# Exchanging score groups and moving a token norm in the written-out order of an attention kernel

## The chip, the cores and the metric

The kernel runs on one core of one Trainium2 chip. The metric is the device time of one execution in microseconds (us); lower is better. Before the change the median of three runs is 799.85 us (798.22 to 801.39).

## What is computed

The input `x` is 4 batches of 2048 tokens with 256 channels, in float32. Two sandwiches are applied, one after the other:

```python
x = x + layernorm(attention(layernorm(x)))
x = x + layernorm(ffn(layernorm(x)))
```

Attention has one head of width 256: `q, k, v = split(x @ weight_qkv)`, scores `q k^T / 16`, a softmax over the 2048 keys, the product with `v`, an output projection and a bias. The second part mixes each token with its predecessor, takes `r = sigmoid(xr W_r)` and `k = relu(xk W_k)^2`, and returns `r * (k W_v)`.

## The kernel before

**Tiling.** The 8192 tokens are cut into 32 blocks of 256 tokens, numbered g, eight to a batch. A block is two tiles of 128 tokens; in most names `j` or `i` is the tile (0 or 1). The keys of a batch are 2048, and scores are made for 128 queries by 1024 keys at a time, so that a block has four score groups: tile `i`, half `h` of the keys. Half 0 comes from the first two chunks of 512 tokens of the batch, half 1 from the other two.

**Precision.** Float32 operands are split into two float16 parts, high and low (`...H` and `...L`), and a product is the sum of three matmuls, or two where one operand has no low part. The weights of q and k are multiplied together ahead of time (`GH`, `GL`), and the first thing made for a block is therefore `t`, the normed tokens times that product.

**Operations.** Each short word in the strings `HEAD`, `LOOP` and `TAIL` calls one small function with a block number. `sM@0/1/0` is `sM` for the current block with tile 1 and half 0; `pj@-2` is `pj` for the block two before. `run` (L914) calls them in the order of the words, and under `manual_schedule` (L922) each engine gets its own instructions in that order. So the string is the order of work of every engine, and of the DMA queue of SP. A word that is written later than another holds up only words on its own engine, and those that wait for its data or its buffer. `HEAD` fills the pipeline, `LOOP` is called for blocks 3 to 26, and `TAIL` empties it.

In one turn of `LOOP` for block g the words that matter here are these.

- Next block's `t`: `tM@1` (TensorE, L350, 10 matmuls into the tile `tps`), `tH@1` (ScalarE, L362, high part), `tL@1` (VectorE, L368, low part `tps - tH`).
- Scores of block g: `sM` (TensorE, L377, 10 matmuls per group, with `tH` and `tL` of the block as the weights that are loaded), `sX` (VectorE, L394, maximum of a group), `sB` (VectorE, L399, the bias of the exponential from the maxima of both halves, so it needs both groups of a tile), `sE` (ScalarE, L406, the exponential and its sum), `sH` (ScalarE, L413), `sL` (VectorE, L419), `sT` (DMA transpose from SP, L425, which writes a quarter of `PT`).
- Product with the values of the block before: `pv@-1/0/8` and `pv@-1/8/16` (TensorE, L432, 40 matmuls each). The first reads the half 0 quarters of `PT`, the second the half 1 quarters. Then `zH` (ScalarE), `zL` (VectorE, L465), which feed `pj` (TensorE, L471), `y` (VectorE, L483), and the statistics `bS` (VectorE), `bP` (GpSimd), the norm `bN` (ScalarE) and `bA` (GpSimd, L526).
- Second part for blocks two to five before: `hF`, `hN`, `hX`, `hT`, `hO`, `hD`, `mk`, `mr`, `kM`, `kR`, `kA`, `uH`, `uL`, `rM`, `rT`, `oM`, `yy`, `dS`, `dP`, `dN`, `dA`, `st`.
- Tokens of blocks ahead: `aS@9` (VectorE, statistics), `aP@9` (GpSimd), `aN@9` (L314, the normed tokens as float16, two instructions of 128x256), `aM@9` and `aD@9` (GpSimd, the low part), `aT@8` (DMA transpose from SP, one turn later).

**Buffers.** Scores lie in two PSUM buffers (`ps_s`), so a group waits until the exponential has read the group that had the buffer before. `tps`, `op`, `k`, `r` and `o` share two more (`ps_m`).

Of the kernel before, what the change touches and what calls it, by code (L numbers as in the profile page):

```python
# [51 lines left out]
sT@2/1/1 pv@1/8/16  # L52
"""
LOOP = """
sM@0/0/0 yy@-5 sM@0/0/1 aS@9 zH@-2 dS@-5 hF@-3/act/act zL@-2 dP@-5 sX@0/0/1 kM@-4 pj@-2 dn@-2
pv@-1/0/8 sX@0/0/0 sB@0/0 hN@-3/act/act y@-2 tM@1 aP@9 sM@0/1/0 dN@-5/act/act sM@0/1/1 aN@9/pool
hX@-3/pool kR@-4 dA@-5/pool aT@8 bS@-2 hC@-3 kA@-4 sE@0/0/0 sE@0/0/1 bP@-2 sH@0/0/0 sH@0/0/1 hT@-3
sL@0/0/0 bN@-2/act/act rM@-4 hO@-3/dve sL@0/0/1 tH@1 aL@11 pv@-1/8/16 hD@-3/pool ld@0 sT@0/0/1
aM@9/pool uH@-4 sX@0/1/0 sX@0/1/1 rT@-4 bA@-2/pool sB@0/1 sE@0/1/0 mk@-3 kH@-3 sH@0/1/0 cS@-2
uL@-4/pool sE@0/1/1 oM@-4 sH@0/1/1 tL@1 sL@0/1/0 sT@0/0/0 mr@-3 sL@0/1/1 st@-5 kL@-3/pool sT@0/1/0  # L60
rH@-3 rL@-3/pool sT@0/1/1 aD@9/pool cP@-2
"""
TAIL_BLOCKS = 5
TAIL = """
# [907 lines left out]
```

## Time and profile before

| | |
|---|---|
| median of three runs | 799.85 us |
| the profiled execution | 798.83 us, of which the profile's span is 797.0 us |
| TensorE (PE) busy | 781.7 us, 98% |
| VectorE (DVE) busy | 696.9 us, 87% |
| ScalarE (ACT) busy | 536.3 us, 67% |
| GpSimd (POOL) busy | 464.6 us, 58% |
| granted TensorE clock, mean | 0.997 |

Times in the profile are counted from the start of the span. A turn of `LOOP` in the middle of the kernel is one period of 23.70 us on every engine; the one from 401.72 to 425.42 us is used as the sample. The first turn (block 3) has its first score matmul near 73 us and the second turn near 93 us; the last turn ends at 638.86 us. In lists of instructions the columns are the start, the length, the engine, the line of the kernel, the operation, output and inputs, shapes and how many were merged; in brackets stands how long the engine sat idle before, and what ended that.

### The profile page before, as it was taken

What the parts mean: (1) busy time and instruction counts of PE and PEld (TensorE: products, weight loads), DVE (VectorE), ACT (ScalarE), POOL (GpSimd) and SP (SyncE); (2) the same over time, 40 slices, a digit from 0 to 9 for tenths busy, and PEclk for the clock granted to TensorE, in tenths of its full rate; (3) what the DMA queues carried; (4) which work ended last, traced back from release to release, by engine and by line L of the source; (5) the groups of instructions that cost most, each with busy time, mean ns of one, the idle gap of its engine ahead of it and who ended that gap; (6) DMA issues with size and microseconds to landing.
All of it is one profiled execution on the core that took longest, in us unless ns stands there. A gap on an engine that the chain in (4) does not pass through costs nothing.

```text
span 797.0 us, 15916 instructions
## 1 busy us (share of the span) xinstructions
PE 781.7 (98%) x5803; PEld 574.3 (72%) x5803; DVE 696.9 (87%) x1606; ACT 536.3 (67%) x889; POOL 464.6 (58%) x632
## 2 busy tenths in 40 slices
PE   8999999999999999999999999999999999999995
PEld 6467677777777777777777777777777767777784
DVE  7998888898888888888888988888898989999977
ACT  6666676686667677667677667668576756575754
POOL 4034457757666766666766766775545534445696
PEclk9999999999999999999999999999999999999998
DMA  8778866556755647664758775656655553655521
GB/s 238 178 146 172 148 153 145 139 133 143 155 141 134 154 119 143 155 157 119 168 117 140 145 169 124 139 118 128 143 123 120 119 119 61 139 122 130 144 71 66
DMA packets 351199, 109.18 MB, mean 137 GB/s; under 512 B 324624, under 2 KB 351120, under 8 KB 351120
## 3 DMA queue, kind: packets, MB, share of 16 engines
q1 hardware_dynamic: 350848, 107.91, 61.1%
q8 instruction: 45, 0.74, 0.4%
q14 instruction: 34, 0.28, 0.1%
q10 hardware_dynamic: 272, 0.26, 0.1%
HBM read 18.75 MB, written 8.39 MB: 34 GB/s over the span
## 4 chain that ended last, share of the span: by engine, by line
PE 90%; DVE 5%; DMA 1%; ACT 1%; issue 1%; POOL 0%; POOLq 0%; SPq 0%; ACTq 0%; DVEq 0%
PE z L442 33%; PE s L173 33%; DMA PT__995<-hl__1240 1%; DMA xa__110<-in_x_dram 1%; PE warm__211 L806 0%; PE op__11019 L173 0%; PE warm__520 L806 0%; PE k__11262 L173 0%; DVE x__10522 L247 0%; DVE sm L818 0%; PE o__11191 L173 0%; PE op__10541 L173 0%; DVE mxmx__10570 L396 0%; DVE pstsA__150 L254 0%; PE r__10479 L173 0%
## 5 line engine op out<-in xcount | busy, mean ns | idle before, releaser
L173 PEld LDWEIGHTS <-w_kH 128*128 128x128 f16 x248 | 24.3, 98 | 8.2 <-issue 0.5
L173 PEld LDWEIGHTS <-GH 128*128 128x128 f16 x192 | 18.8, 98 | 3.7 <-DVE tL__334 L372 0.7
L442 PEld LDWEIGHTS <-X__271 128*128 128x128 f16 x160 | 15.7, 98 | 2.2
L442 PEld LDWEIGHTS <-X__6669 128*128 128x128 f16 x160 | 15.7, 98 | 2.2
L442 PEld LDWEIGHTS <-X__5273 128*128 128x128 f16 x160 | 15.6, 98 | 2.2
L442 PEld LDWEIGHTS <-X__189 128*128 128x128 f16 x160 | 15.5, 98 | 2.3 <-issue 0.5
L442 PEld LDWEIGHTS <-X__233 128*128 128x128 f16 x160 | 15.7, 98 | 1.8
L442 PEld LDWEIGHTS <-X__718 128*128 128x128 f16 x160 | 15.7, 98 | 1.8
L442 PEld LDWEIGHTS <-X__324 128*128 128x128 f16 x160 | 15.7, 98 | 1.8
L442 PEld LDWEIGHTS <-X__4575 128*128 128x128 f16 x160 | 15.7, 98 | 1.8
L442 PEld LDWEIGHTS <-X__571 128*128 128x128 f16 x160 | 15.7, 98 | 1.8
L442 PEld LDWEIGHTS <-X__1783 128*128 128x128 f16 x160 | 15.7, 98 | 1.8
L442 PEld LDWEIGHTS <-X__3179 128*128 128x128 f16 x160 | 15.7, 98 | 1.8
L442 PEld LDWEIGHTS <-X__7367 128*128 128x128 f16 x160 | 15.7, 98 | 1.8
L442 PEld LDWEIGHTS <-X__3877 128*128 128x128 f16 x160 | 15.7, 98 | 1.8
L442 PEld LDWEIGHTS <-X__1141 128*128 128x128 f16 x160 | 15.7, 98 | 1.8
L442 PEld LDWEIGHTS <-X__2481 128*128 128x128 f16 x160 | 15.7, 98 | 1.8
L442 PEld LDWEIGHTS <-X__5971 128*128 128x128 f16 x160 | 15.6, 98 | 1.8
L173 PEld LDWEIGHTS <-GL 128*128 128x128 f16 x128 | 12.5, 98 | 3.4 <-issue 0.9
L173 PEld LDWEIGHTS <-w_kL 128*128 128x128 f16 x124 | 12.1, 98 | 1.4
L329 POOL TENSOR_TENSOR X__718<-xa__485,X__718 128x256 f16<-128x256 f32 x1 | 1.7, 1657 | 16.4 <-ACT xa__485 L271 16.4
L273 POOL TENSOR_SCALAR xa__344<-xa__344,rsrna__455,nmrna__456 128x128 f32<-128x128 f32 x2 | 0.9, 449 | 17.2 <-ACT X__571 L271 17.2
(3619 smaller groups left out, 3383.6 us busy)
## 6 DMA issues: line engine op xcount, KB each, us to landing
xa__103<-in_x_dram SPq DMA_DIRECT2D x1, 256.0 KB, 3.3
scr_wk__101<-in_wkT_dram ACTq DMA_DIRECT2D x1, 256.0 KB, 3.8
xa__110<-in_x_dram SPq DMA_DIRECT2D x1, 256.0 KB, 4.2
xa__112<-in_x_dram SPq DMA_DIRECT2D x1, 256.0 KB, 4.5
scr_wq__114<-in_wqT_dram SPq DMA_DIRECT2D x1, 256.0 KB, 4.7
scr_wv__130<-in_wvT_dram SPq DMA_DIRECT2D x1, 256.0 KB, 4.9
xa__163<-in_x_dram SPq DMA_DIRECT2D x1, 256.0 KB, 5.2
xa__175<-in_x_dram SPq DMA_DIRECT2D x1, 256.0 KB, 5.4
```

The lines of the kernel that those rows point to most:

```text
L173: nc.tensor.matmul(out_ap, l, r, start=(i == 0), stop=(i == len(pairs) - 1))
L273: eng(e).tensor_scalar(dst, src, rs[:, j:j + 1], nm[:, j:j + 1], ALU.mult, ALU.add)
L329: eng(e).tensor_tensor(Xh[:, :, 2, :], T["xa", g][:, :, P:D], Xh[:, :, 1, :], ALU.subtract)
L442: nc.tensor.matmul(z[:, int(c), 0:QB], a, p, start=(kt == 0 and n == 0), stop=(kt == KT - 1 and n == len(prs) - 1))
```

## The change

Only the string `LOOP` differs. The numbers of words and of instructions of each kind are the same; `aN@9` goes from GpSimd to VectorE.

- `sM@0/0/1` comes before `sM@0/0/0`, ahead of `yy`. The order of `sX` is as it was.
- `hF@-3` comes before `dS@-5`; they are on ScalarE and VectorE.
- `sM@0/1/0` moves ahead of `hN@-3`, `sB`, `y@-2` and `tM@1`. On TensorE it passes `tM@1`.
- `aN@9/pool` becomes `aN@9/dve`, between `y@-2` and `bS@-2` on VectorE.
- `sE@0/0/0` moves up, but stays where it was on ScalarE. `dA@-5` moves behind `hC@-3`, both on GpSimd.
- `bN@-2` moves in the string and keeps its place on ScalarE.
- `tL@1` moves from behind `sX`, `sB`, `mk` and `cS` to ahead of `sX@0/1/0` on VectorE.
- `aM@9` moves behind `bA@-2` on GpSimd, ahead of `uL@-4` as before.

```diff
 LOOP = """
-sM@0/0/0 yy@-5 sM@0/0/1 aS@9 zH@-2 dS@-5 hF@-3/act/act zL@-2 dP@-5 sX@0/0/1 kM@-4 pj@-2 dn@-2
-pv@-1/0/8 sX@0/0/0 sB@0/0 hN@-3/act/act y@-2 tM@1 aP@9 sM@0/1/0 dN@-5/act/act sM@0/1/1 aN@9/pool
-hX@-3/pool kR@-4 dA@-5/pool aT@8 bS@-2 hC@-3 kA@-4 sE@0/0/0 sE@0/0/1 bP@-2 sH@0/0/0 sH@0/0/1 hT@-3
-sL@0/0/0 bN@-2/act/act rM@-4 hO@-3/dve sL@0/0/1 tH@1 aL@11 pv@-1/8/16 hD@-3/pool ld@0 sT@0/0/1
-aM@9/pool uH@-4 sX@0/1/0 sX@0/1/1 rT@-4 bA@-2/pool sB@0/1 sE@0/1/0 mk@-3 kH@-3 sH@0/1/0 cS@-2
-uL@-4/pool sE@0/1/1 oM@-4 sH@0/1/1 tL@1 sL@0/1/0 sT@0/0/0 mr@-3 sL@0/1/1 st@-5 kL@-3/pool sT@0/1/0
-rH@-3 rL@-3/pool sT@0/1/1 aD@9/pool cP@-2
+sM@0/0/1 sM@0/0/0 yy@-5 aS@9 zH@-2 hF@-3/act/act dS@-5 zL@-2 dP@-5 sX@0/0/1 kM@-4 pj@-2 dn@-2
+pv@-1/0/8 sX@0/0/0 sM@0/1/0 hN@-3/act/act sB@0/0 y@-2 tM@1 aP@9 dN@-5/act/act sM@0/1/1 aN@9/dve
+hX@-3/pool kR@-4 sE@0/0/0 aT@8 bS@-2 hC@-3 kA@-4 dA@-5/pool sE@0/0/1 bP@-2 sH@0/0/0 sH@0/0/1 hT@-3
+sL@0/0/0 rM@-4 hO@-3/dve sL@0/0/1 bN@-2/act/act tH@1 aL@11 pv@-1/8/16 tL@1 hD@-3/pool ld@0 sT@0/0/1
+uH@-4 sX@0/1/0 sX@0/1/1 rT@-4 bA@-2/pool sB@0/1 sE@0/1/0 mk@-3 kH@-3 sH@0/1/0 cS@-2 aM@9/pool
+uL@-4/pool sE@0/1/1 oM@-4 sH@0/1/1 sL@0/1/0 sT@0/0/0 mr@-3 sL@0/1/1 st@-5 kL@-3/pool sT@0/1/0 rH@-3
+rL@-3/pool sT@0/1/1 aD@9/pool cP@-2
 """
```

On the queue of SP the transposes and loads keep their order. On ScalarE the order is the same throughout.

## The prediction

> **What bounds the kernel now.** I read the page's busy times first, then the busy time in stretches, then the waits, then one period of the repeated part engine by engine. TensorE is the bound, and the stretches tell where it is not:
>
> ```profile
> PE 781.7 (98%) x5803; PEld 574.3 (72%) x5803; DVE 696.9 (87%) x1606; ACT 536.3 (67%) x889; POOL 464.6 (58%) x632
> 401.72:425.42 23.70, 23.70 (x181) 17.42 (x179) 20.58 (x49) 16.48 (x28) 15.71 (x21) 1.00 0.71 142
> 92.92:117.50 24.58, 24.20 (x181) 17.35 (x179) 21.78 (x44) 18.02 (x30) 14.18 (x19) 1.00 0.65 127
> 117.50:638.86 521.36, 521.36 (x3919) 383.22 (x3917) 453.99 (x1031) 362.77 (x594) 332.08 (x435) 1.00 0.62 138
> ```
>
> The stretches' columns are the window, its length, then busy time and count of PE, PEld, DVE, ACT, POOL, the granted clock, DMA share and GB/s. From 117.50 to 638.86 us TensorE has no gap at all. A busy matmul engine could still run slowly, so I check its spacing. Score matmuls start every 0.2155 us (413 to 418 us), those of 256 columns every 0.109 us. A turn issues 40 of the first (8.63 us) and 80 + 48 + 10 of the second (15.06 us): 23.69 us, the whole period of 23.70. So in the steady turns nothing can be gained by order; a new order can only leave it or open gaps. The idle of 797.0 - 781.7 = 15.3 us lies in the head, in the tail and, 0.38 us of it, in the second turn (TensorE's, VectorE's and ScalarE's lists, and the DMA's piece of the chain that ended last):
>
> ```profile
> 98.66 0.27 PE L173 MATMUL op__1330<-w_oL,Hzp__1309 128*128 128x256 f16 x1
> 99.02 0.28 PE L173 MATMUL op__1330<-w_oH,Lzp__1310 128*128 128x256 f16 x1
> 100.58 0.60 PE L442 MATMUL z<-PT__995,X__189 128*128 128x256 f16 x4 [0.29 <-DMA PT__995<-hl__1240]
> 88.76 1.23 DVE L396 TENSOR_REDUCE mxmx__1118<-s 128x1 f32<-128x1024 f32 x1 [0.25 <-PE s L173]
> 90.41 1.20 ACT L409 ACTIVATE p__1232<-s,bb__1230,esc 128x1024 f32<-128x1024 f32 x1 [3.62 <-DVE bb__1230 L403]
> 94.56 5.88 DMA PT__995<-hl__1240
> ```
>
> There `pj` starts its third matmul 0.25 us later than the spacing (99.02 against 98.77), for zL, and `pv` waits for the quarter of PT that left at 94.56. Both go back to the exponential at 90.41, which waited for the bias. So the first turn is a chain without slack, the others have some.
>
> **The steady turn, part by part.** Times are in the sample period, whose scores start at 401.72.
>
> ```profile
> 406.58 1.22 DVE L396 TENSOR_REDUCE mxmx__5794<-s 128x1 f32<-128x1024 f32 x1
> 413.25 1.23 DVE L422 SCALAR_TENSOR_TENSOR hl__5999<-p__5991,hl__5999 128x1024 f16<-128x1024 f32 x1 [0.97 <-ACT hl__5999 L416]
> 416.47 1.23 DVE L396 TENSOR_REDUCE mxmx__5946<-s 128x1 f32<-128x1024 f32 x1 [0.26 <-PE s L173]
> 418.63 1.23 DVE L396 TENSOR_REDUCE mxmx__5946<-s 128x1 f32<-128x1024 f32 x1 [0.93 <-PE s L173]
> 415.04 0.58 ACT L365 ACTIVATE tH__6023<-tps__5931 128x512 f16<-128x512 f32 x1
> 419.94 0.69 ACT L671 ACTIVATE th__6079<-r__6008,sc 128x512 f32<-128x512 f32 x1 [3.81 <-PE r__6008 L173]
> 410.99 1.19 ACT L409 ACTIVATE p__5993<-s,bb__5923,esc 128x1024 f32<-128x1024 f32 x1
> 410.25 1.28 POOL L723 TENSOR_TENSOR x__4324<-x__4324,y__5807 128x512 f32<-128x512 f32 x1
> 415.15 1.95 POOL L595 TENSOR_TENSOR dd__6067<-hT__5988 128x512 f32<-128x512 f32 x1 [2.47 <-DMA x__6069<-in_x_dram]
> ```
>
> Exchange of the first two groups: same matmuls, 4.32 us in all. VectorE reaches its first maximum at 406.58 only, after zL, when both groups had ended at 406.04; so the maxima, the bias (409.48) and the exponentials keep their times. Cost nothing; the cover is VectorE's own queue. If that were 2 us earlier, the other order would show. The buffers: the first two groups still follow the exponentials of the last two (read by 398.1 and 400.8, needed at 401.7 and 403.9), 3.1 us spare at least.
>
> `sM@0/1/0` ahead of `tM`: that group starts at 413.02 instead of 414.11. It takes the buffer of half 0 of the first tile, whose exponential starts at 409.79 and gives its accumulator by 411.08: 1.9 us spare. Even the other buffer (410.99 plus 1.28, so 412.27) would be free. `tM` ends 2.16 us later, at 416.27 instead of 414.11; it needs its buffer from y (410.45), far earlier.
>
> The low half of `t`: ScalarE starts 0.20 us behind the last matmul of a group (r ends 419.74, th starts 419.94), so `tH` goes from 415.04 to 416.47. Queued behind it are uH (0.5 us, wanted by uL, which GpSimd reaches at 419.2) and th at 419.94: covered. `tL` can start at 416.47 + 0.58 + 0.03 = 417.08, VectorE idle until then (sL ends near 416.13), and takes 0.60, measured from its start to the next one's. The two maxima behind it go to 417.68 and, 1.14 later, 418.82; the second was at 418.63. The bias is thus 0.19 late, and allows the exponential at 420.47 (0.39 from bias start to exponential start at 90.02 and 90.41, on 420.08). ScalarE is not free before 420.53, because th waits for r. So the delay dies there with 0.06 us to spare. In the old place tL took 0.60 us ahead of a sL that then sat idle for 0.51 waiting for ScalarE; taking it away gains nothing. `oM` now waits for tL (417.68) but runs at 424.1.
>
> What is late next, if it does not die: sH, sL, mr, sL, yy, aS, dS, zL on the two engines, and zL's result is ready near 406.6 against 407.46, when TensorE loads it. That is 0.88 us more, 0.94 in all. The transposes of PT leave at 424.66 and land 3.8 later, 428.5, against 432.3: wider.
>
> The norm on VectorE: two instructions of 128x256. In the head the same pair runs there at 67.80 with the next start at 68.45, so 0.65 us; on GpSimd it takes 1.09. It stands behind y at 410.45 and has its inputs (407.97). It pushes bS and kA by 0.65 into the 0.97 us in which VectorE waits for sH until 413.25: cost nothing, 0.32 left. At GpSimd's 1.09 it would push 0.12, into the wait for tH. Behind bS wait bP and bN on ScalarE: bS at 412.25, bP 0.98 later, bN starts at 414.06 in any case. I take 0.65, the same engine and shape. GpSimd is 1.09 us ahead from there: hX, hT's transpose, `aL` and `ld` leave earlier on SP, whose queue is idle between 406.3 and 410.32. They load what is used at 414.39 or a turn later, so nothing gained. `dA` behind `hC` shifts 0.2 us; `aM` behind `bA` swaps 0.85 with 1.26 us, and uL behind both stays. The sum of a steady turn: 0.
>
> Contention has no row of this exact pair. Its low end is 0. Its high end is a stretch of the same shape on GpSimd: 1.95 against 1.28 us above, 0.67. I take 0: GpSimd would run dA (409.4 to 410.7) beside the norm, and even 0.67 longer it is done before bP, which waits for bS until 412.25. [...]
>
> **The first turn.** Here there is no th, so the delay goes through. `tM` goes from 83.31-84.40 to 85.47-86.56, tH to 86.76, tL to 87.37, the maxima to 87.97 and 89.11 against 88.76: +0.35 us. The bias, the exponential at 90.41, sH, sL and the transpose at 94.56 follow by 0.35, and so do zL and the landing, so that `pv` starts at 100.93. Bounds: if the two waits there (0.25 and 0.41 us, from 100.17 to 100.58) vanished, -0.66; with a stretch of 0.67 on top, +1.02. I take +0.35, the rows' own sum. From there on TensorE is solid and carries it to the tail, whose order is unchanged; the last three turns have no norm, as blocks end at 31.
>
> **Sum.** 798.83 + 0.35 = 799.2 us for the profiled execution. The median of the runs is 1.02 above that execution, so I forecast 800.2. About 0.5% (4 us) is what a measurement of this kernel can tell from no change.
>
> [...]
>
> **Rivals.**
> - *No change of note* (forecast): -0.66 to +1.02 around the median, 799.2 to 800.9, and the spread of runs.
> - *Slower: zL late for pj.* Decides when the second maximum is over 0.94 us later than reckoned. For it: only 0.06 dies at th, and VectorE is 87% busy. Against: the 0.88 behind it. Two stretches of 0.67, on tL and one maximum, give 1.34 - 0.94 = 0.40 us on each of 23 turns, 9 us: 809. If only the 0.65 of the norm came on top of everything, still no wait.
> - *Faster: a gap closes.* The most is the 0.66 us of the second turn; for 4 us the tail's order of arrival would have to change too, and its words are the same and TensorE has no gap from 638.86 to 755. It gives 799.2, or 794 with part of the tail.
> - *The change does not do what it says.* `sM@0/1/0` finds its buffer late; by the times above it does not, and 800.2 stays.
>
> **How the numbers follow.** Forecast with small gains and the last rival 0.86; slower by zL 0.10; faster by over 4 us 0.04. The likeliest case alone, with the runs' spread of 1.6 us, is 798 to 802.5. The range reaches part of the way to the slower case, up to 803.5, and to 797.5 below; about a tenth is left out above and less below. Chances: faster 0.04, same 0.86, slower 0.10.
>
> **What would show it.** Right: a period of 23.70 us with TensorE full; tH near 416.5 and tL near 417.1 in the sample; VectorE idle before tL, not before the second maximum; the pair of L273 at 0.65 us; first bias near 90.4 and `pv` near 100.9. Wrong: a wait of pj on DVE, or of a score group on ACT, in every turn; a period over 23.8; the tail's chain ending otherwise.

## The result and the profile after

The changed kernel takes 803.51 us (median of six runs, 803.34 to 805.20) against 799.39 us (six runs, 798.22 to 801.39) before: a ratio of 1.0059, 95% interval 1.0049 to 1.0069. It is slower by about 4.1 us; 800.2 had been forecast.

The head of the page and two stretches of the profile after. A stretch's columns are window, length, then busy time and count of PE, PEld, DVE, ACT, POOL, the granted clock, DMA share and GB/s.

```profile
span 803.4 us, 15879 instructions
PE 785.6 (98%) x5803; PEld 574.7 (72%) x5803; DVE 745.7 (93%) x1646; ACT 542.9 (68%) x889; POOL 440.3 (55%) x592
401.92:425.93 24.01, 23.88 (x180) 17.32 (x179) 23.39 (x52) 16.80 (x27) 14.45 (x20) 1.00 0.66 135
117.50:638.86 521.36, 519.32 (x3876) 377.74 (x3875) 495.74 (x1059) 365.14 (x589) 308.52 (x398) 1.00 0.62 137
```

A turn takes 24.01 us where it took 23.70, and TensorE, which had no gap between 117.5 and 638.86 us, now has some. VectorE is busy for 23.39 of the 24.01 us; before it was 20.58 of 23.70. The norm that was moved to it explains 0.65 of the 2.81 us between them.

This is the gap in TensorE's list, in the sample turn, with the same wait in the chain of waits (engine, line, releaser, us in total, times, longest):

```profile
411.95 0.27 PE L173 MATMUL op__5863<-w_oL,Hzp__5829 128*128 128x256 f16 x1
412.35 0.28 PE L173 MATMUL op__5863<-w_oH,Lzp__5830 128*128 128x256 f16 x1
PEld L173 <- DVE Lzp__5830 L467: 0.4, 1, 0.4
```

The third matmul of `pj` starts 0.40 us after the second instead of 0.11: it waits 0.29 us for `zL`. That happens in 15 turns, those of blocks 8 to 22: 15 x 0.29 = 4.35 us. From block 23 on, where no norm of a later block is left, a turn takes 23.70 us again. In the profiled execution the tail starts 6.38 us later than before; the other 2.0 us lie ahead of the first turn, and belong to that execution (805.2 us, the longest of the six) and not to the change.

So why is `zL` late? VectorE's list in the sample turn:

```profile
411.61 0.68 DVE L467 SCALAR_TENSOR_TENSOR Lzp__5830<-z,Hzp__5829 128x512 f16<-128x512 f32 x1
412.21 1.21 DVE L396 TENSOR_REDUCE mxmx__5794<-s 128x1 f32<-128x1024 f32 x1
413.53 1.22 DVE L479 TENSOR_SCALAR ds__5876<-ds__5876,two 128x2 f32<-128x2 f32 x1
414.87 1.20 DVE L396 TENSOR_REDUCE mxmx__5794<-s 128x1 f32<-128x1024 f32 x1
417.08 0.73 DVE L273 TENSOR_SCALAR X__5971<-xa__5327,rsrna__5954,nmrna__5955 128x256 f16<-128x256 f32 x2
422.75 0.69 DVE L372 SCALAR_TENSOR_TENSOR tL__6067<-tps__5943,tH__6023 128x512 f16<-128x512 f32 x1
423.35 2.35 DVE L396 TENSOR_REDUCE mxmx__5923<-s 128x1 f32<-128x1024 f32 x2
425.93 1.69 DVE L600 SCALAR_TENSOR_TENSOR mk__6086<-dd__6069,mus,hT__5989 128x256 f32<-128x256 f32 x2
428.53 1.00 DVE L204 TENSOR_SCALAR vesc__6096<-mvsc__6095,sc 128x2 f32<-128x2 f32 x1
```

GpSimd's, over the same time:

```profile
411.71 0.70 POOL L213 TENSOR_TENSOR rsrnd__5845<-vesd__5837,nhalf 128x2 f32<-128x2 f32 x1 [0.38 <-DVE vesd__5837 L208]
413.57 1.16 POOL L558 TENSOR_TENSOR hh__5832<-h__5935,hh__5832 128x512 f16<-128x512 f32 x1
425.79 1.15 POOL L276 TENSOR_TENSOR Lup__6075<-ka__5975,Hup__6074 128x512 f16<-128x512 f32 x1
428.35 1.16 POOL L276 TENSOR_TENSOR Lkp__6090<-mk__6086,Hkp__6089 128x512 f16<-128x512 f32 x1 [1.41 <-ACT Hkp__6089 L164]
```

The same instructions in the kernel before, VectorE's list, then GpSimd's:

```profile
407.89 0.23 DVE L479 TENSOR_SCALAR ds__5876<-ds__5876,two 128x2 f32<-128x2 f32 x1
420.08 0.91 DVE L600 SCALAR_TENSOR_TENSOR mk__6086<-dd__6067,mus,hT__5988 128x256 f32<-128x256 f32 x2
421.91 0.23 DVE L204 TENSOR_SCALAR vesc__6096<-mvsc__6095,sc 128x2 f32<-128x2 f32 x1
```

```profile
408.08 1.09 POOL L273 TENSOR_SCALAR X__5971<-xa__5327,rsrna__5942,nmrna__5943 128x256 f16<-128x256 f32 x2
409.13 1.16 POOL L558 TENSOR_TENSOR hh__5841<-h__5925,hh__5841 128x512 f16<-128x512 f32 x1
419.17 1.15 POOL L276 TENSOR_TENSOR Lup__6075<-ka__5975,Hup__6074 128x512 f16<-128x512 f32 x1
```

Three instructions of VectorE that the change does not touch have grown, and each ends just behind a two-input operation of GpSimd. L479 (the denominators of the softmax times a scale, in `dn`, two numbers per partition) went from 0.23 to 1.22 us and ends at 414.75; `hX` on GpSimd ends at 414.73. The pair of `mk` went from 0.91 to 1.69 us; its first half is held and ends at 427.22, 0.28 us behind `uL` (426.94). L204 went from 0.23 to 1.00 us and ends at 429.53; `kL` ends at 429.51. Over the window 300 to 420 us, five turns, the busy time of L479 is 6.09 us (before 1.14), that of `mk` and `mr` together 12.80 (8.87), that of L204 4.99 (1.14): per turn 0.99, 0.79 and 0.77 us more. (With the norm's 0.65 that makes 3.20 us, 0.39 more than VectorE's busy time grew by; where the 0.39 went was not followed up.)

The collision of L479 is no accident of phase. The same instruction on VectorE, L208 of the statistics `dS`, releases both sides. On VectorE `zL`, a maximum and the sum of the denominators (L478) follow it, and L479 starts 1.92 us after `zL` (411.61 to 413.53). On GpSimd four small operations follow it, and the next one starts 1.86 us after the first of them (411.71 to 413.57). Before, that next one was the norm `aN` (408.08 to 409.17), and `hX` came behind it when L479 had long passed (407.89 to 408.12). Now it is `hX`. In 19 of the 20 turns with a norm the two sides meet and L479 takes 1.21 to 1.25 us; the exception is block 4. From block 5 on it is held in each of them and starts every 24.0 us (125.40, 149.41, 173.41), while TensorE keeps its 23.70 until block 8, where its gap opens: the time to spare between the two was used up first.

The theory that the experiments test: taking the norm off GpSimd lets `hX` start about 1.2 us sooner, beside L479 (1.86 us behind GpSimd's first small operation instead of 3.05, 406.08 to 409.13, before); VectorE is held there, falls behind, and `mk` meets `uL` as well. The rivals: the norm's own 0.65 us on VectorE; the new order, above all `tL` ahead of the maxima; and, as to the kind of collision, any instruction of VectorE at that place or only those of a certain form.

### The profile page after: what moved, and what is told of

Its sections match the earlier page's. It is cut to its first block, busy times and chain, and to the rows that moved or that the text cites. A ratio compares the mean times of both kernels' runs of the same rounds, so it can differ in the third digit from the quotient of the medians.

```text
span 803.4 us, 15879 instructions
## 1 busy us (share of the span) xinstructions
PE 785.6 (98%) x5803; PEld 574.7 (72%) x5803; DVE 745.7 (93%) x1646; ACT 542.9 (68%) x889; POOL 440.3 (55%) x592
## 4 chain that ended last, share of the span: by engine, by line
DVE 46%; PE 38%; issue 10%; ACT 5%; DMA 1%; POOL 0%; SPq 0%; POOLq 0%; DVEq 0%; ACTq 0%
PE z L442 14%; PE s L173 13%; DMA xa__163<-in_x_dram 1%; PE warm__211 L806 0%; DVE mxmx__6970 L396 0%; DVE mxmx__6621 L396 0%; DVE mxmx__5574 L396 0%; DVE mxmx__5225 L396 0%; DVE mxmx__3480 L396 0%; DVE mxmx__2433 L396 0%; DVE mxmx__7319 L396 0%; DVE mxmx__6272 L396 0%; DVE mxmx__5923 L396 0%; DVE mxmx__4876 L396 0%; DVE mxmx__4527 L396 0%
```

## The experiments

Every kernel here does all the work. Ratios are to runs of the kernel before on the same chip (medians 798.76 to 798.98 us), with a 95% interval.

**1. The changed kernel with the norm back on GpSimd, and 2. the kernel before with only the norm moved.**

The first, against the changed kernel:

```diff
-pv@-1/0/8 sX@0/0/0 sM@0/1/0 hN@-3/act/act sB@0/0 y@-2 tM@1 aP@9 dN@-5/act/act sM@0/1/1 aN@9/dve
+pv@-1/0/8 sX@0/0/0 sM@0/1/0 hN@-3/act/act sB@0/0 y@-2 tM@1 aP@9 dN@-5/act/act sM@0/1/1 aN@9/pool
```

The second, against the kernel before:

```diff
-pv@-1/0/8 sX@0/0/0 sB@0/0 hN@-3/act/act y@-2 tM@1 aP@9 sM@0/1/0 dN@-5/act/act sM@0/1/1 aN@9/pool
+pv@-1/0/8 sX@0/0/0 sB@0/0 hN@-3/act/act y@-2 tM@1 aP@9 sM@0/1/0 dN@-5/act/act sM@0/1/1 aN@9/dve
```

> The changed order with the token norm aN back on GpSimd, at the same word. Theory A (collision: without aN, GpSimd starts the split hX where VectorE starts the 128x2 instruction of dn at L479, which is then held to the end of hX): L479 back to 0.23 us, mk (L600) and the epsilon instruction (L204) back to about 0.42 and 0.23, period 23.70, time 799.4 to 800.2. Theory B (the order itself: tL ahead of the two maxima makes the second bias late): L479 0.23, but the period stays near 24.0 and the time near 803.5. Theory C (the 0.65 us of the norm on VectorE is what fills it): as A, 799.4 to 800.2.

> The kernel before with only the norm aN moved to VectorE. Theory A: L479 lasts 1.2 us in every turn that has a norm, VectorE's idle of 2.8 us a turn shrinks by about 1.6 or more; period 23.7 to 24.0, time 800 to 804. Theory B: no loss without the moved tL, 799.4, period 23.70, whatever L479 lasts. Theory C: L479 0.23, and 0.65 us more busy a turn fits the idle, 799.4.

Measured: the first takes 798.64 us, 0.9995 (0.9985 to 1.0004), with L479 at 0.229 us and a period of 23.70. The second takes 808.75 us, 1.0123 (1.0106 to 1.0140), with L479 at 1.22, L204 at about 1.0; the holds came as expected, but the time lies above the 800 to 804 us that went with them. So the norm's move alone carries the whole loss, and more than the whole change shows: the rest of the change takes more than half of it back. The rest by itself costs and gains nothing.

**3. The changed kernel with `dA` ahead of `hX` on GpSimd.** The norm stays on VectorE; `dA`, which there waits 0.89 us for ScalarE, keeps `hX` away from L479.

```diff
-hX@-3/pool kR@-4 sE@0/0/0 aT@8 bS@-2 hC@-3 kA@-4 dA@-5/pool sE@0/0/1 bP@-2 sH@0/0/0 sH@0/0/1 hT@-3
+dA@-5/pool hX@-3/pool kR@-4 sE@0/0/0 aT@8 bS@-2 hC@-3 kA@-4 sE@0/0/1 bP@-2 sH@0/0/0 sH@0/0/1 hT@-3
```

> The changed order, norm still on VectorE, with the addition dA ahead of hX on GpSimd. dA waits for ScalarE some 0.7 us, so GpSimd stands idle when L479 runs. Theory A: L479 0.23 us, L600 and L204 back too or nearly, period 23.70, 799.4 to 800.5. Theory B: period near 24.0, 803.5. Theory C: norm still costs VectorE its 0.65 us, period near 24.0, 803.

Measured: 798.69 us, 0.9996 (0.9987 to 1.0006), L479 at 0.23, period 23.70. The loss is gone although VectorE still does the norm. `hX` now lies beside the norm itself, and that pair is stretched (VectorE's list of this kernel):

```profile
410.09 1.28 DVE L273 TENSOR_SCALAR X__5971<-xa__5327,rsrna__5954,nmrna__5955 128x256 f16<-128x256 f32 x2
```

It takes 1.28 instead of 0.73 us, and costs nothing there, because VectorE has waits behind it: `hl`, which waited 0.32 us in the changed kernel, now waits for nothing, and `tL` still starts after 0.75 us of idle time.

**4. The kernel before with GpSimd's norm moved behind `hX`.** VectorE gets no work at all; only `hX` runs sooner.

```diff
-pv@-1/0/8 sX@0/0/0 sB@0/0 hN@-3/act/act y@-2 tM@1 aP@9 sM@0/1/0 dN@-5/act/act sM@0/1/1 aN@9/pool
-hX@-3/pool kR@-4 dA@-5/pool aT@8 bS@-2 hC@-3 kA@-4 sE@0/0/0 sE@0/0/1 bP@-2 sH@0/0/0 sH@0/0/1 hT@-3
+pv@-1/0/8 sX@0/0/0 sB@0/0 hN@-3/act/act y@-2 tM@1 aP@9 sM@0/1/0 dN@-5/act/act sM@0/1/1
+hX@-3/pool aN@9/pool kR@-4 dA@-5/pool aT@8 bS@-2 hC@-3 kA@-4 sE@0/0/0 sE@0/0/1 bP@-2 sH@0/0/0 sH@0/0/1 hT@-3
```

> The kernel before, norm still on GpSimd, with hX ahead of aN on GpSimd; nothing else moves. It makes the collision alone. Theory A: L479 1.2 us in every turn with a norm, though VectorE got no work; the turn has room for about 1 us, so period 23.70 to 23.8 and 799.4 to 801.5. Theories B and C: L479 0.23 us, 799.4.

Measured: 809.19 us, 1.0127 (1.0112 to 1.0142), period 24.30, again far above the time expected from the collision (799.4 to 801.5). VectorE's list, then GpSimd's:

```profile
403.68 2.09 DVE L600 SCALAR_TENSOR_TENSOR mk__5737<-dd__5718,mus,hT__5639 128x256 f32<-128x256 f32 x2
416.18 1.22 DVE L479 TENSOR_SCALAR ds__5876<-ds__5876,two 128x2 f32<-128x2 f32 x1
```

```profile
402.92 1.27 POOL L528 TENSOR_TENSOR x__5022<-x__5022,y__5579 128x512 f32<-128x512 f32 x1
404.15 1.34 POOL L276 TENSOR_TENSOR Lup__5726<-ka__5625,Hup__5725 128x512 f16<-128x512 f32 x1
416.22 1.16 POOL L558 TENSOR_TENSOR hh__5841<-h__5925,hh__5841 128x512 f16<-128x512 f32 x1
417.36 1.10 POOL L273 TENSOR_SCALAR X__5972<-xa__5327,rsrna__5942,nmrna__5943 128x256 f16<-128x256 f32 x2
```

This is the cleanest run against the rival that blames the norm's own time: nothing was added to VectorE, and the loss is the same 10 us as in experiment 2. Here the pair of `mk` starts inside `bA`, and both halves are held: the first ends 0.28 us behind `bA`, the second 0.28 us behind `uL`, 2.09 us in all.

**5. The changed kernel with the norm on GpSimd, behind `hX`, `hC` and `dA`.**

```diff
-pv@-1/0/8 sX@0/0/0 sM@0/1/0 hN@-3/act/act sB@0/0 y@-2 tM@1 aP@9 dN@-5/act/act sM@0/1/1 aN@9/dve
-hX@-3/pool kR@-4 sE@0/0/0 aT@8 bS@-2 hC@-3 kA@-4 dA@-5/pool sE@0/0/1 bP@-2 sH@0/0/0 sH@0/0/1 hT@-3
+pv@-1/0/8 sX@0/0/0 sM@0/1/0 hN@-3/act/act sB@0/0 y@-2 tM@1 aP@9 dN@-5/act/act sM@0/1/1
+hX@-3/pool kR@-4 sE@0/0/0 aT@8 bS@-2 hC@-3 kA@-4 dA@-5/pool aN@9/pool sE@0/0/1 bP@-2 sH@0/0/0 sH@0/0/1 hT@-3
```

> The changed order with the norm back on GpSimd, but behind hX, hC and dA, so that hX still starts beside L479. Theory A: L479 1.2 us in every turn with a norm, and since the norm's own 0.65 us on VectorE lay in a wait for ScalarE, taking it away changes nothing: period near 24.0, 803 to 804. Theory C (the norm's time on VectorE has its share): period 23.70, 799 to 800, even with L479 at 1.2.

Measured: 803.36 us, 1.0049 (1.0034 to 1.0064), the time of the changed kernel without the norm on VectorE. Where the norm had been, VectorE waits: `hl` there starts after 0.98 us of idle time for ScalarE, against 0.32 us in the changed kernel. The norm's 0.65 us lies in a wait, as forecast, even now that VectorE is late.

**6. The changed kernel with L479 done as two columns.**

```diff
-        nc.vector.tensor_scalar(ds, ds, sig["w_o"], None, ALU.mult)
+        for j in range(2):
+            nc.vector.tensor_scalar(ds[:, j:j + 1], ds[:, j:j + 1], sig["w_o"], None, ALU.mult)
```

> The changed kernel whole, with the one 128x2 instruction at L479 replaced by two of 128x1, as the bias instruction is (0.27 us beside hX before). Theory A1 (what is held is the kind of VectorE instruction: two elements or more from and to SBUF, by tensor_scalar): neither of the two is held, 0.2 to 0.3 us each, period 23.70, 799 to 800. Theory A2 (whatever VectorE runs beside the start of hX is held): one of the two, or the reciprocal behind them, takes 1.0 to 1.2 us, period near 24.0, 803.5.

Measured: 798.88 us, 1.0002 (0.9992 to 1.0011), period 23.70, TensorE full. The two columns run right beside `hX` (VectorE's list, then GpSimd's):

```profile
407.36 0.33 DVE L480 TENSOR_SCALAR ds__5891<-ds__5891,two 128x1 f32<-128x1 f32 x2
```

```profile
407.39 1.15 POOL L559 TENSOR_TENSOR hh__5847<-h__5951,hh__5847 128x512 f16<-128x512 f32 x1
```

The neighbour on GpSimd and the place are those of the changed kernel, the same two numbers per partition are multiplied, and nothing is held. It is the form of the instruction that collides: 128x2 waits 0.99 us, 128x1 twice does not. The 128x2 reciprocal behind it takes its 0.17 us inside `hX` too. One edit of a line repairs the whole loss.

**7. The kernel before with only the two score groups exchanged, and 8. with only `tL` moved.**

Run 7, against the kernel before:

```diff
-sM@0/0/0 yy@-5 sM@0/0/1 aS@9 zH@-2 dS@-5 hF@-3/act/act zL@-2 dP@-5 sX@0/0/1 kM@-4 pj@-2 dn@-2
-pv@-1/0/8 sX@0/0/0 sB@0/0 hN@-3/act/act y@-2 tM@1 aP@9 sM@0/1/0 dN@-5/act/act sM@0/1/1 aN@9/pool
+sM@0/0/1 sM@0/0/0 yy@-5 aS@9 zH@-2 dS@-5 hF@-3/act/act zL@-2 dP@-5 sX@0/0/1 kM@-4 pj@-2 dn@-2
+pv@-1/0/8 sX@0/0/0 sM@0/1/0 sB@0/0 hN@-3/act/act y@-2 tM@1 aP@9 dN@-5/act/act sM@0/1/1 aN@9/pool
```

Run 8, against the kernel before:

```diff
-sL@0/0/0 bN@-2/act/act rM@-4 hO@-3/dve sL@0/0/1 tH@1 aL@11 pv@-1/8/16 hD@-3/pool ld@0 sT@0/0/1
+sL@0/0/0 bN@-2/act/act rM@-4 hO@-3/dve sL@0/0/1 tH@1 aL@11 pv@-1/8/16 tL@1 hD@-3/pool ld@0 sT@0/0/1
...
-uL@-4/pool sE@0/1/1 oM@-4 sH@0/1/1 tL@1 sL@0/1/0 sT@0/0/0 mr@-3 sL@0/1/1 st@-5 kL@-3/pool sT@0/1/0
+uL@-4/pool sE@0/1/1 oM@-4 sH@0/1/1 sL@0/1/0 sT@0/0/0 mr@-3 sL@0/1/1 st@-5 kL@-3/pool sT@0/1/0
```

> The kernel before with the two exchanges of score groups alone (second half first, and the third group ahead of tM); tL, aM, aN as before. Theory A: no wait of TensorE in the steady turns, period 23.70, 799 within 0.8. Rival: the score buffers or the later tM open a gap in each turn, 0.1 us of it making 801.5.

> The kernel before with tL alone moved ahead of the two maxima on VectorE; tM is still ahead of the third group, so that tL waits for nothing much. Theory A: period 23.70, 799 within 0.8, L479 0.23. Rival (Theory B, the bias late by tL): period over 23.75, 800.5 or more.

Measured: 798.74 us, 0.9999 (0.9989 to 1.0008), and 798.74 us, 0.9996 (0.9987 to 1.0005). Neither does anything to an undisturbed kernel. In run 7 L204 is held too (17.60 us for 15 of them, 1.17 each), and so is the pair of `mk`, both without loss: holds by themselves need not cost anything. VectorE's list of run 7, in the sample turn:

```profile
419.69 1.40 DVE L600 SCALAR_TENSOR_TENSOR mk__6086<-dd__6067,mus,hT__5988 128x256 f32<-128x256 f32 x2
422.00 1.18 DVE L204 TENSOR_SCALAR vesc__6096<-mvsc__6095,sc 128x2 f32<-128x2 f32 x1
```

**9 and 10. Experiment 4 with one more part of the change: `tL` early (9), the score groups (10).** The question is which part took half of the loss back.

Run 9, against the kernel of experiment 4:

```diff
-sL@0/0/0 bN@-2/act/act rM@-4 hO@-3/dve sL@0/0/1 tH@1 aL@11 pv@-1/8/16 hD@-3/pool ld@0 sT@0/0/1
+sL@0/0/0 bN@-2/act/act rM@-4 hO@-3/dve sL@0/0/1 tH@1 aL@11 pv@-1/8/16 tL@1 hD@-3/pool ld@0 sT@0/0/1
...
-uL@-4/pool sE@0/1/1 oM@-4 sH@0/1/1 tL@1 sL@0/1/0 sT@0/0/0 mr@-3 sL@0/1/1 st@-5 kL@-3/pool sT@0/1/0
+uL@-4/pool sE@0/1/1 oM@-4 sH@0/1/1 sL@0/1/0 sT@0/0/0 mr@-3 sL@0/1/1 st@-5 kL@-3/pool sT@0/1/0
```

Run 10, against the kernel of experiment 4:

```diff
-sM@0/0/0 yy@-5 sM@0/0/1 aS@9 zH@-2 dS@-5 hF@-3/act/act zL@-2 dP@-5 sX@0/0/1 kM@-4 pj@-2 dn@-2
-pv@-1/0/8 sX@0/0/0 sB@0/0 hN@-3/act/act y@-2 tM@1 aP@9 sM@0/1/0 dN@-5/act/act sM@0/1/1
+sM@0/0/1 sM@0/0/0 yy@-5 aS@9 zH@-2 dS@-5 hF@-3/act/act zL@-2 dP@-5 sX@0/0/1 kM@-4 pj@-2 dn@-2
+pv@-1/0/8 sX@0/0/0 sM@0/1/0 sB@0/0 hN@-3/act/act y@-2 tM@1 aP@9 dN@-5/act/act sM@0/1/1
```

> The kernel before with GpSimd's norm moved behind the split of h (the order that gave 809.2 us and a period of 24.30) and the low half of t ahead of the maxima. If the moved low half of t is what makes the collision cheaper in the changed kernel (803.5, period 24.01): the mask pair is held less, about 0.77 us over its own 0.84 instead of 1.2, period 23.9 to 24.05, time 802.5 to 804.5. If it has no part in that: period 24.3, 807.5 to 810. L479 is held to about 1.22 us either way.

> The kernel before with GpSimd's norm moved behind the split of h (809.2 us, period 24.30) and both exchanges of score groups, the low half of t where it was. If the exchanges are what makes the collision cheaper in the changed kernel: period 23.9 to 24.05, time 802.5 to 804.5. If they have no part in it: period 24.3, 807.5 to 810. L479 is held to about 1.22 us either way.

Measured: 804.61 us, 1.0071 (1.0054 to 1.0088), and 808.53 us, 1.0122 (1.0106 to 1.0138). It is `tL`. With it early the pair of `mk` reaches VectorE 0.13 us after `uL` has started (400.37 and 400.24) and is held 0.8 us; without it, the pair comes while `bA` still runs and is held through both, 1.2 us. So `tL` ahead of the maxima, worthless in a kernel without the collision, halves the loss in one that has it.

**11 and 12. The statistics L204 and L208 of block c as columns, in the changed kernel (11) and in the kernel of experiment 4 (12).** By now I had a sum: three holds per turn, 0.99 + 0.79 + 0.77 = 2.55 us, and a period 0.31 us longer, so a loop with 2.24 us to spare.

```diff
-            nc.vector.tensor_scalar(ve[:, 0, cut(js)], mv[:, cut(js), 1], EPS, hs2, ALU.add, ALU.mult)
+            for j in map(int, js):
+                nc.vector.tensor_scalar(ve[:, 0, j:j + 1], mv[:, j:j + 1, 1], EPS, hs2, ALU.add, ALU.mult)
...
-        if nm:
+        for j in map(int, js if nm and k == "c" else ""):
+            nc.vector.tensor_scalar(ve[:, 1, j:j + 1], mv[:, j:j + 1, 0], -1.0, None, ALU.mult)
+        if nm and k != "c":
```

> The changed kernel with the two 128x2 instructions of L204 and L208 for the statistics of block c done as 128x1 columns (all the work is done). If the loss is a sum, holds of L479 0.99, mask pair 0.79 and L204 0.77 against about 2.24 us that the loop over VectorE and ScalarE has to spare, then without the 0.77 and with some 0.25 for two more instructions the sum is 2.03 us: period 23.70, TensorE full, 798.3 to 799.7, although L479 is still held to about 1.22. If the hold of L479 alone decides (it is the one that the change starts): the period stays near 24.0, 802.5 to 804.

> The kernel with GpSimd's norm moved behind the split of h (809.2 us, period 24.30), with the same two instructions as columns. By the sum: holds 0.99 + 1.18 plus 0.25 for the added instructions is 2.42 against 2.34 to spare in that order: period 23.7 to 23.85, 799 to 802. If the hold of L479 alone decides: period near 24.3, 807 to 810.

Measured: 803.44 us, 1.0052 (1.0037 to 1.0068), with the period still 24.01, and 800.13 us, 1.0012 (1.0003 to 1.0022), with a period of 23.80. The second came as the sum said; the first did not, and the sum falls with it: L204's hold cost nothing in the changed kernel. VectorE's list of run 11 shows why:

```profile
424.31 1.69 DVE L603 SCALAR_TENSOR_TENSOR mk__6116<-dd__6099,mus,hT__6019 128x256 f32<-128x256 f32 x2
426.80 0.33 DVE L205 TENSOR_SCALAR vesc__6126<-mvsc__6125,sc 128x1 f32<-128x1 f32 x2
427.64 1.33 DVE L425 SCALAR_TENSOR_TENSOR hl__6122<-p__6114,hl__6122 128x1024 f16<-128x1024 f32 x1 [0.39 <-ACT hl__6122 L419]
429.92 1.23 DVE L425 SCALAR_TENSOR_TENSOR hl__6153<-p__6138,hl__6153 128x1024 f16<-128x1024 f32 x1 [0.15 <-ACT hl__6153 L419]
```

L204 (here L205) is free, and VectorE now waits 0.39 and 0.15 us for ScalarE instead. ScalarE casts the result of `mk` first (`kH`), and what it must do behind that is late by the hold of `mk`. The two branches behind `mk` are of nearly the same length: the second `hl` starts 5.61 us after `mk` here (424.31 to 429.92) and 5.60 us in the changed kernel (401.92 to 407.52). In the order of run 12 `tL` still lies on VectorE's branch, and that branch is the longer one: in run 4 `hl` follows `tL` with no idle time (407.66 and 408.26). Taking L204's hold from it pays.

**13. The changed kernel with `aM` behind `kL` on GpSimd.** It moves `uL` 0.87 us forward, away from `mk`, and leaves L479 beside `hX`.

```diff
-uH@-4 sX@0/1/0 sX@0/1/1 rT@-4 bA@-2/pool sB@0/1 sE@0/1/0 mk@-3 kH@-3 sH@0/1/0 cS@-2 aM@9/pool
-uL@-4/pool sE@0/1/1 oM@-4 sH@0/1/1 sL@0/1/0 sT@0/0/0 mr@-3 sL@0/1/1 st@-5 kL@-3/pool sT@0/1/0 rH@-3
+uH@-4 sX@0/1/0 sX@0/1/1 rT@-4 bA@-2/pool sB@0/1 sE@0/1/0 mk@-3 kH@-3 sH@0/1/0 cS@-2
+uL@-4/pool sE@0/1/1 oM@-4 sH@0/1/1 sL@0/1/0 sT@0/0/0 mr@-3 sL@0/1/1 st@-5 kL@-3/pool aM@9/pool sT@0/1/0 rH@-3
```

> The changed kernel with aM behind kL on GpSimd, so that uL starts 0.87 us sooner and its span no longer covers the mask pair; kL waits 1.4 us for ScalarE anyway, and aM fits behind it. If L479's 0.99 us costs time only together with the 0.79 us that the mask pair is then held: L479 stays at 1.22, the mask pair falls from 1.69 to 0.87 to 1.05, period 23.70, 798.3 to 799.7. If L479's hold alone is enough to lengthen the period: 24.0 again, 802.5 to 804.5.

Measured: 798.30 us, 0.9996 (0.9986 to 1.0005), period 23.70. VectorE's list:

```profile
407.33 1.22 DVE L479 TENSOR_SCALAR ds__5876<-ds__5876,two 128x2 f32<-128x2 f32 x1
419.73 0.87 DVE L600 SCALAR_TENSOR_TENSOR mk__6086<-dd__6069,mus,hT__5989 128x256 f32<-128x256 f32 x2
421.51 0.23 DVE L204 TENSOR_SCALAR vesc__6096<-mvsc__6095,sc 128x2 f32<-128x2 f32 x1
```

And `uL` in GpSimd's list of run 13, then `mk` and `uL` in run 6:

```profile
418.73 1.16 POOL L276 TENSOR_TENSOR Lup__6075<-ka__5975,Hup__6074 128x512 f16<-128x512 f32 x1
```

```profile
419.75 0.87 DVE L601 SCALAR_TENSOR_TENSOR mk__6102<-dd__6085,mus,hT__6005 128x256 f32<-128x256 f32 x2
418.73 1.16 POOL L276 TENSOR_TENSOR Lup__6091<-ka__5991,Hup__6090 128x512 f16<-128x512 f32 x1
```

L479 is held in full, in the same 19 turns, and the kernel is as fast as the one before. Together with run 6 (no hold of L479: no hold of the others, no loss) this settles how the loss comes about in the changed kernel: the hold of L479 starts it, and it takes time only because it brings `uL` and `mk` together. It is `uL` that moves. In run 6 it starts 1.02 us ahead of `mk` and is nearly over when `mk` comes; in the changed kernel it starts 0.14 us ahead (425.79 and 425.93). `hO` on VectorE (L570) is late by the hold, and GpSimd's `hD`, `bA`, `aM` and `uL` run one behind the other after it; `mk` is late by less, because VectorE's wait ahead of `tL` (0.79 us in run 6) takes up most of the hold. None of the runs beats the kernel before by more than the interval.

## Why the prediction was wrong

**What held.** "So in the steady turns nothing can be gained by order": runs 1, 3, 6 and 8 end at 798.6 to 798.9 us with the period of 23.70. The exchange of the first two groups and `sM@0/1/0` ahead of `tM` cost nothing (run 7). `tL` comes where it was put: in run 1 it starts at 417.03 (forecast 417.08), the maxima behind it at 417.63 (417.68), and the delay dies as said. "I take 0.65" for the norm on VectorE: it starts at 417.08 and the next instruction at 417.73, and run 5 shows that it lies in the wait for `sH`. The tail keeps its order and carries the delay.

**The first turn.** "I take +0.35" was not met. Run 1 is 0.20 us late in the head already, which the change does not touch (its first `pv` starts at 45.93 against 45.73). Less these 0.20 us, the exponential came 0.17 us late (90.78 against 90.41), the third matmul of `pj` 0.18 us late (99.40 against 99.02), and `pv` 0.28 us early (100.50 against 100.58), since its wait for `PT` closed. The forecast had taken the start of `tM` from the chain of waits (83.31) and the other times from the lists, where `tM` starts at 83.15; with that its own sum gives 0.19 for the bias. That the wait for `PT` would close stood only among its bounds. All of this is below what these runs can tell in the time.

**What failed.** The failing step is the last part of the norm's move: "GpSimd is 1.09 us ahead from there: hX, hT's transpose, `aL` and `ld` leave earlier on SP [...] so nothing gained". The gain was rightly put at nothing; the cost was not looked at. I asked what the earlier operations would release, and not what they would then run beside. The trace after shows it: `hX` runs beside L479, `zL` comes late, and `pj` waits 0.29 us in 15 turns. With it failed the term for contention: "Its low end is 0", the high end 0.67, "I take 0". It was sought at the wrong place (the moved norm, on VectorE, stretching `dA` on GpSimd) and in one direction only. Measured, it is 0.99 us on L479 and, behind that, 0.79 us on `mk`, both on VectorE; it falls on instructions the change never names, from an operation of GpSimd that only moved up. The pair that I did consider never met: in the changed kernel `dA` is over at 416.08 and the norm starts at 417.08. Beside another neighbour, `hX`, the norm is stretched by 0.55 us (run 3), and that is hidden. (A slip without weight: "the last three turns have no norm" should be four, blocks 23 to 26.)

**The rival that came true.** "Slower: zL late for pj" names the place and the wait. Its cause, two stretches on `tL` and a maximum, is not what the trace shows: neither is stretched (`tL` takes 0.69 us and the two maxima behind it 2.35 together; in run 13, which loses nothing, 0.68 and 2.35). Its price was 0.40 us on 23 turns, 9 us; measured are 0.29 us on 15. I gave it one chance in ten because the margin behind the second maximum looked wide, 0.94 us. Two holds that I had put at nothing make 1.78 us per turn; L479's 0.99 alone costs no time (run 13). That the rival named the right wait is in part luck.

**It could be read before.** The lists of the kernel before had everything. Take `aN` from GpSimd, and `hX` moves to about 408.0 us, right against L479 at 407.89. And one turn there shows what then happens, in the lists of VectorE and of GpSimd:

```profile
97.62 0.17 DVE L206 TENSOR_SCALAR vesa__1302<-mvsa__1301 128x2 f32<-128x2 f32 x1
97.69 0.68 DVE L208 TENSOR_SCALAR vesa__1302<-mvsa__1301 128x2 f32<-128x2 f32 x1
```

```profile
97.68 0.67 POOL L329 TENSOR_TENSOR X__1141<-xa__908,X__1141 128x256 f16<-128x256 f32 x1
```

The same 128x2 form, 0.17 us when alone, takes 0.68 beside an operation of GpSimd, and ends with it. More than that: the three holds themselves stand in the kernel before, in two of its last four turns (blocks 24 and 26), where GpSimd has no norm any more. There `hX` and `dA` run beside L478 and L479, and TensorE stays full. Block 24, VectorE's list, then GpSimd's:

```profile
574.38 1.20 DVE L479 TENSOR_SCALAR ds__8285<-ds__8285,two 128x2 f32<-128x2 f32 x1
586.16 1.42 DVE L600 SCALAR_TENSOR_TENSOR mk__8483<-dd__8466,mus,hT__8389 128x256 f32<-128x256 f32 x2
588.49 1.00 DVE L204 TENSOR_SCALAR vesc__8493<-mvsc__8492,sc 128x2 f32<-128x2 f32 x1
```

```profile
574.29 1.26 POOL L723 TENSOR_TENSOR x__6767<-x__6767,y__8225 128x512 f32<-128x512 f32 x1
585.75 1.15 POOL L276 TENSOR_TENSOR Lup__8472<-ka__8377,Hup__8471 128x512 f16<-128x512 f32 x1
588.31 1.16 POOL L276 TENSOR_TENSOR Lkp__8487<-mk__8483,Hkp__8486 128x512 f16<-128x512 f32 x1 [1.41 <-ACT Hkp__8486 L164]
```

"Contention has no row of this exact pair" was true of the norm beside `dA`, but the rows that would have given the price stood in the lists.

What the three holds have in common is their end: in the changed kernel L479 and L204 end 0.02 us after GpSimd's operation, the first half of `mk` 0.28 us after it. At the place of L479 the form matters too: one instruction of 128x2 takes 1.22 us there, two of 128x1 take 0.33 us together (run 6). What makes one engine wait for the other no run shows, nor why L479 is the one that waits (see the end). The prediction had weighed contention for the norm alone.

## What to carry to other kernels

An operation taken off an engine's queue lets what stands behind it start sooner (here `hX`, by 1.2 us): list what each of these will now run beside on the other engine, as one lists what it will release; here the two were GpSimd and VectorE. Where both queues were released by the same instruction, the collision kept coming (in 19 of 20 turns), and the hold on a tiny instruction was nearly as long as the neighbour's operation (0.99 us beside 1.16). Whether it cost anything depended on the next link of the loop, so a cheap change of form (128x2 into two of 128x1: run 6, 798.88 us) or of place (`aM` behind `kL`: run 13, 798.30 us) took the whole loss away.

## What the runs showed that I had not expected

- The smallest instruction was hit hardest: L479 handles two numbers per partition and went from 0.23 to 1.22 us, five times as long. Two larger ones, which read PSUM, kept their times beside GpSimd's operations: a maximum took 1.20 us beside `dA` (414.87; 1.21 in the kernel before), `tL` 0.69 beside `hD` (422.75; 0.68 before).
- In the records L479 starts 0.03 to 0.04 us ahead of `hX` (413.53 and 413.57; 416.18 and 416.22 in run 4) and is the one held all the same. Why the one with the earlier start is held, no run settles.
- GpSimd's operations can be stretched as well. In run 13 the pair of `aM` takes 2.25 us beside `hl`, which starts 0.23 us ahead of it (422.70 and 422.93), and `mr`, against 0.87 before; in that place nothing waits for it. GpSimd's list of run 13:

```profile
422.93 2.25 POOL L273 TENSOR_SCALAR xa__5327<-xa__5327,rsrna__5954,nmrna__5955 128x128 f32<-128x128 f32 x2
```

- The same hold of 0.77 us on L204 was worth nothing in one order (run 11) and most of 10 us in the other (run 12, 809.19 to 800.13). Between two branches of nearly equal length the size of a hold says little; the order decides which branch is the longer.
